# A transformer block on one core: the second MLP product with high and low weights side by side, and a batch's preparation spread over four chunk steps

## The chip, the cores and the metric

The kernel runs on one core of a Trainium2 chip. The metric is the device time of one execution in microseconds. Three executions of the kernel before gave 762.52 to 766.37 us, median 764.86.

The engines are called PE (TensorE; PEld is its loading of weights, the stationary operand), DVE (VectorE), ACT (ScalarE), POOL (GpSimd) and SP (SyncE, which here only issues DMAs). SBUF is the on-chip working memory, PSUM the memory in which matmuls accumulate; one PSUM bank holds 512 f32 columns per partition.

## What is computed

One block of a diffusion transformer for 16 batches of 256 tokens with 256 features: modulated self-attention, cross-attention to a context, and a modulated MLP with 1024 hidden features. The change touches only the MLP, which is the end of the reference:

```python
x = x + c_attn_out                                   # after cross-attention
x_norm2 = modulate(_ln(x), shift_m, scale_m)         # layernorm, times (1 + scale), plus shift
h = jax.nn.gelu(x_norm2 @ W_mlp1 + b_mlp1)           # 256 -> 1024, tanh form
h = h @ W_mlp2 + b_mlp2                              # 1024 -> 256
x = x + gate_m[:, None] * h
return x
```

All values are f32. The kernel multiplies in a reduced f32 format (fp32r) and gets the accuracy back by splitting: a value is a high part, rounded to the format, and a low part, the rest. A product a·b is then three matmuls: high·high, high·low and low·high.

## The kernel before

The attention of all batches comes first, as a pipeline of 32 units (16 self, 16 cross), written out by hand as steps (`beat`, L1037). Its results lie in DRAM as `x2d`. The last units run beside the start of the MLP; the order of that stretch is given by the lists in `E_` (L55), where `'M'` says at which half step the first three batches are loaded, biased, normalised and turned (L1003 to L1005).

After the attention, a loop over 64 chunks does the MLP (L1173 to L1193): 16 batches b of four chunks c, each chunk 256 hidden features. One round of that loop, the chunk step of (b, c), issues in this order, i being the chunk's number:

- `mlp_gelu` of chunk i + 1 (L837): ACT applies GELU twice to the first product in PSUM, into `hf` (f32, tag "pt", five buffers) and into `hh` (fp32r, the high part, three buffers); POOL subtracts into `hl`, the low part (three buffers)
- if c is 0, `mlp_T` of batch b + 1 (L800): PE turns the normalised tile `xn` by four transposes (`psT_m` in the trace), DVE scales into `xTf_m`, ACT writes the high part (into `wkch` or `wqch`, weights no longer needed), DVE subtracts into the low part (`wkcl`, `wqcl`)
- `mlp_first` of chunk i + 2 (L824): 12 matmuls of 256 columns into `ph`
- `mlp_second` of chunk i - 1 (L852): for each of two token tiles t, two 128-wide pieces of the hidden features and three matmuls, 12 in all, each with 128 x 128 stationary (a piece of `hh` or `hl`) and 256 columns of weights streaming. They accumulate over the batch's four chunks in `m.po`, the first 256 columns of a bank; batches alternate between the banks `sp` and `st`. In the trace these are `s<-big,hh`, `st<-big,hl` and so on. After a batch's last chunk, DVE multiplies the two tiles by the gate (`mt`), adds `xg` (`y`), and SP stores it
- at c = 1: `mlp_bias`, `mlp_stats` and `mlp_apply` of batch b + 2 (L1185 to L1188): POOL adds a bias to the loaded tile (`x<-x,cb`); DVE takes mean and variance (`st_m`, `mv_m`); POOL adds epsilon and takes the power -0.5 (`rs_m`, two small instructions, L289); DVE subtracts and multiplies (`xn_m`, two instructions of 256 columns, one per token tile)
- at c = 2: `mlp_residual` of b (L792): SP fetches the gate and gated bias (`gm`), DVE adds the latter to the tile (`xmg`)
- at c = 3: `mlp_load` of b + 3 (L775)

PE, DVE, POOL and SP issue in the order in which the program is written (L57, L58); ACT does so until chunk 23 and is ordered by the scheduler after that (L1174). So an instruction that waits holds up everything behind it on its engine.

The weights of the second product lie in `big[2]` (L871): eight pieces of 256 columns of high parts, then eight of low parts, so the high and low part of one piece lie 8 KB apart in each partition:

```python
W2 = [big[2][:, 0], big[2][:, 1]]
```

In the profile, nearly all instructions carry L51, the line of the helper that issues them, so they are told apart by their tiles.

Of the kernel before, what the change touches and what calls it, by code (L numbers as in the profile page):

```python
# [10 lines left out]
F32 = mybir.dt.float32  # L11
F32R = mybir.dt.float32r
AF = mybir.ActivationFunctionType
ALU = mybir.AluOpType
AX = mybir.AxisListType

P = 128
# [4 lines left out]
def pixart_block(  # L22
# [8 lines left out]
    B, N, H = x.shape  # L31
# [3 lines left out]
    NT = N // P  # L35
# [21 lines left out]
    PE = InOrder(nc.tensor, True)  # L57
    ACT, DVE, POOL, SP = (InOrder(e, True) for e in (nc.scalar, nc.vector, nc.gpsimd, nc.sync))  # L58

    const = ctx.enter_context(tc.tile_pool(name="const", bufs=1))  # L60
    work = ctx.enter_context(tc.tile_pool(name="work", bufs=2))
# [23 lines left out]
    big = [const.tile([P, 2, 8, N], F32R, name=f"big{i}") for i in range(3)]  # L85
# [15 lines left out]
    def tok(ap, b):  # L101
        return ap[b].rearrange("(t p) h -> p t h", p=P)
# [33 lines left out]
    st = psum.tile([P, 2, 512], F32, tag="st", name="st", bufs=1)  # L136
    sp = [psum.tile([P, 512], F32, tag=f"s{r}", name=f"s{r}", bufs=1) for r in range(2)]
# [134 lines left out]
    def layernorm(src, name):  # L272

        o = Box()

        def stats():
            o.st = work.tile([P, NT, 6], F32, tag="bnst", name=f"st_{name}")
            for t in range(NT):
                DVE.bn_stats(o.st[:, t], src()[:, t])

        def rstd(power=True):
            o.mv = work.tile([P, NT, 2], F32, tag="bnmv", name=f"mv_{name}")
            for t in range(NT):
                DVE.bn_aggr(o.mv[:, t], o.st[:, t])
            o.rs = work.tile([P, NT], F32, tag="rstd", name=f"rs_{name}")
            if power:
                o.pow()

        def pow():  # L289
            POOL.tensor_scalar(o.rs, o.mv[:, :, 1], EPS, None, ALU.add)  # L290
            POOL.tensor_tensor(o.rs, o.rs, mhalf, ALU.pow)

        def apply(eng=E_['LN'].get(name[0])):
            o.xn = work.tile([P, NT, H], F32, tag="xn", name=f"xn_{name}", bufs=3)
            if eng == "act":
                nb = work.tile([P, NT], F32, tag="nb", name=f"nb_{name}")
                DVE.scalar_tensor_tensor(nb, o.mv[:, :, 0], -1.0, o.rs, ALU.mult, ALU.mult)
            for t in range(NT):
                if eng == "act":
                    ACT.activation(o.xn[:, t], src()[:, t], AF.Identity, bias=nb[:, t:t + 1],  # L300
                                   scale=o.rs[:, t:t + 1])
                else:
                    (DVE if eng == "dve" else POOL).tensor_scalar(
                        o.xn[:, t], src()[:, t], o.mv[:, t, 0:1], o.rs[:, t:t + 1],
                        ALU.subtract, ALU.mult)

        o.steps, o.pow = [stats, rstd, apply], pow
        return o
# [103 lines left out]
    def mm3_tok(dst, xT, t, W, kn=KC, start=True, stop=True):  # L412
        n = 0
        for k in range(kn):
            for a, b in ((xT[0], W[0]), (xT[0], W[1]), (xT[1], W[0])):
                PE.matmul(dst, a[:, k, t * P:(t + 1) * P], b[:, k],
                          start=(start and n == 0), stop=(stop and n == 3 * kn - 1))
                n += 1
# [132 lines left out]
    def bc_t(ap):  # L551
        return ap.unsqueeze(1).to_broadcast([P, NT, H])
# [107 lines left out]
    def side(home, r):  # L660
        return home[r] if isinstance(home, (list, tuple)) else home[:, r]
# [111 lines left out]
    M = {}  # L773

    def mlp_load(b):  # L775
        m = M[b] = Box()
        m.h, m.hT = {}, {}
        m.xt = work.tile([P, NT, H], F32, tag="x", name=f"x2_{b}", bufs=5)
        SP.dma_start(m.xt, tok(X2d, b))
        m.ln = layernorm(lambda: m.xt, f"m{b}")  # L780

    def mlp_bias(b):
        POOL.tensor_tensor(M[b].xt, M[b].xt, bc_t(cb), ALU.add)

    def mlp_stats(b):
        M[b].ln.steps[0]()
        M[b].ln.steps[1]()

    def mlp_apply(b):
        M[b].ln.steps[2]("dve")  # L790

    def mlp_residual(b):  # L792
        m = M[b]
        m.g = work.tile([P, 2, H], F32, tag="g", name=f"gm_{b}", bufs=3)
        SP.dma_start(m.g.rearrange("p a h -> p (a h)"),
                     gd[b, 2:4].rearrange("a h -> (a h)").partition_broadcast(P))
        m.xg = work.tile([P, NT, H], F32, tag="xg", name=f"xmg_{b}")
        DVE.tensor_tensor(m.xg, m.xt, bc_t(m.g[:, 1]), ALU.add)

    def mlp_T(b):  # L800

        m = M[b]
        pst = ps_gen(f"psT_m{b}", SHORT)
        for f in range(KC):
            for t in range(NT):
                PE.transpose(pst[:, f * N + t * P:f * N + (t + 1) * P],
                             m.ln.xn[:, t, f * P:(f + 1) * P], ident)
        y = work.tile([P, KC, N], F32, tag="y", name=f"xTf_m{b}", bufs=2)
        hi, lo = (Wkc, Wqc)[b % 2]
        for f in range(KC):  # L810
            DVE.tensor_scalar(y[:, f], pst[:, f * N:(f + 1) * N], sc1[:, 1, f, b:b + 1],
                              cpT[:, 6 + f, b:b + 1], ALU.mult, ALU.add)
        if b in E_['DV']:
            DVE.tensor_copy(hi, y)
        else:
            for f in range(KC):
                ACT.activation(hi[:, f], pst[:, f * N:(f + 1) * N], AF.Identity,
                               bias=cpT[:, 6 + f, b:b + 1], scale=sc1[:, 1, f, b:b + 1])
        DVE.tensor_tensor(lo, y, hi, ALU.subtract)
        m.xT = (hi, lo)  # L820

    NCH = NF // 2
# [14 lines left out]
    def mlp_gelu(b, c):  # L837
        ph = M[b].h.pop(c)
        hf = work.tile([P, 2, N], F32, tag="pt", name=f"hf_{b}_{c}", bufs=5)
        hh = work.tile([P, 2, N], F32R, tag="qkh", name=f"hh_{b}_{c}", bufs=3)  # L840
        hl = work.tile([P, 2, N], F32R, tag="qkl", name=f"hl_{b}_{c}", bufs=3)
        for dst in (hf, hh):
            if b == 0:
                ACT.activation(dst, ph, AF.Gelu_apprx_tanh)
                continue
            for j in range(2):
                f = BM1 + 2 * c + j
                ACT.activation(dst[:, j], ph[:, j], AF.Gelu_apprx_tanh, bias=bT[:, f:f + 1])
        POOL.tensor_tensor(hl, hf, hh, ALU.subtract)
        M[b].hT[c] = (hh, hl)  # L850

    def mlp_second(b, c):  # L852
        m = M[b]
        hT = m.hT.pop(c)
        if c == 0:
            m.po = [side((sp, st)[b % 2], t)[:, :H] for t in range(NT)]
        for t in range(NT):
            mm3_tok(m.po[t], hT, t, [W2[0][:, 2 * c:2 * c + 2], W2[1][:, 2 * c:2 * c + 2]],
                    kn=2, start=(c == 0), stop=(c == NCH - 1))
        if c == NCH - 1:  # L860
            t1 = work.tile([P, NT, H], F32, tag="t1", name=f"mt_{b}")
            for t in range(NT):
                DVE.tensor_tensor(t1[:, t], m.po[t], m.g[:, 0], ALU.mult)
            y = work.tile([P, NT, H], F32, tag="x1", name=f"y_{b}", bufs=5)
            DVE.tensor_tensor(y, m.xg, t1, ALU.add)
            SP.dma_start(tok(out, b), y)


# [2 lines left out]
    W2 = [big[2][:, 0], big[2][:, 1]]  # L871
# [128 lines left out]
    def end(p, f, *a):  # L1000
        at_end[p // 16 - 1, p % 16].append(lambda: f(*a))

    for b, ps in enumerate(E_['M']):  # L1003
        for p, f in zip(ps, (mlp_load, mlp_bias, mlp_stats, mlp_apply, mlp_T)):
            end(p, f, b)  # L1005
    for c, p in enumerate(E_['H']):
        end(p, mlp_first, 0, c, (("c", 2), ("x1", 5))[c // 2])
# [165 lines left out]
    for i, (b, c) in enumerate(chunks):  # L1173
        ACT.on = i < E_['AP']  # L1174
        if i + 1 < len(chunks):
            mlp_gelu(*chunks[i + 1])
        if c == 0 and 0 < b < B - 1:
            mlp_T(b + 1)
        if i > 3 and i + 2 < len(chunks):
            mlp_first(*chunks[i + 2])  # L1180
        if i > 0:
            mlp_second(*chunks[i - 1])
        for _, f in zip(range(1), pst):
            f()
        if c == 1 and 2 < b + 2 < B:  # L1185
            mlp_bias(b + 2)
            mlp_stats(b + 2)
            mlp_apply(b + 2)  # L1188
        if c == 2:
            mlp_residual(b)  # L1190
        if c == 3 and b + 3 < B:
            mlp_load(b + 3)
    mlp_second(*chunks[-1])  # L1193


# [46 lines left out]
```

## Time and profile before

| what | value |
|---|---|
| median of three executions | 764.86 us (762.52 to 766.37) |
| the profiled execution | 765.13 us |
| its span, first to last instruction | 763.3 us |
| granted TensorE clock, mean | 0.999 |
| PE busy | 748.3 us, 10048 matmuls |
| DVE, ACT, POOL busy | 579.9, 563.3, 533.7 us |

The span is shorter than the execution's time by what lies around the first and last instruction. In rows of instructions stand: start and length in us (or a count and a mean), the engine, the operation, output<-inputs by name, the shape (for PE: contraction rows * output columns of the stationary operand, then partitions x columns), the count, and in brackets how long the engine was idle before and who released it. In rows of the chain of waits stand start, length and what ran.

### The profile page before, as it was taken

The page shows a single profiled execution, that of the slowest core. Times are in us where ns is not written, and L with a number is a line of the kernel's source. Part 1 is how long each engine was busy: PE and PEld are TensorE (multiplying, and loading weights), DVE is VectorE, ACT ScalarE, POOL GpSimd, SP SyncE. Part 2 cuts the span into 40 slices and gives each one's busy share as a digit, 9 for nine tenths or more (in the row PEclk, how much of TensorE's full clock was granted, in tenths as well). Part 3 has the DMA queues.
Part 4 walks back from the last instruction along what each step waited for, and adds up shares of the span by engine and source line. Part 5 has one row for each costly group of instructions (what it writes and reads, how often), then busy time and mean ns, then how long its engine had stood idle before and what let it go on. Part 6 is the DMA issues. An engine that isn't in the chain of part 4 may idle for free.

```text
span 763.3 us, 25123 instructions
## 1 busy us (share of the span) xinstructions
PE 748.3 (98%) x10048; PEld 653.4 (86%) x10048; DVE 579.9 (76%) x1214; ACT 563.3 (74%) x973; POOL 533.7 (70%) x553
## 2 busy tenths in 40 slices
PE   9999999999999999999999999999899999999997
PEld 8788878888888888888888888777689999999997
DVE  4888988888888888888888888887764565656652
ACT  4278888888888888888888888887657666666663
POOL 6767768696776968769687898854557666575653
PEclk9999999999999999999999999999999999999999
DMA  6554445436445354554545555445112222121211
GB/s 207 147 158 130 134 120 148 123 93 172 120 130 140 111 157 119 141 145 116 141 110 166 159 150 151 116 115 154 58 58 57 64 62 83 43 83 49 77 51 49
DMA packets 89049, 87.98 MB, mean 115 GB/s; under 512 B 8610, under 2 KB 84676, under 8 KB 88932
## 3 DMA queue, kind: packets, MB, share of 16 engines
q1 hardware_dynamic: 88468, 85.58, 40.0%
q8 instruction: 80, 1.31, 0.7%
q0 software_dynamic: 192, 0.52, 0.3%
q14 instruction: 37, 0.30, 0.1%
q10 hardware_dynamic: 272, 0.26, 0.1%
HBM read 26.97 MB, written 8.46 MB: 46 GB/s over the span
## 4 chain that ended last, share of the span: by engine, by line
PE 75%; DVE 9%; POOL 7%; ACT 6%; issue 1%; DMA 1%; POOLq 0%; ACTq 0%; DVEq 0%
PE o L51 15%; PE s L51 13%; PE st L51 11%; PE ps_qc L51 5%; DVE xn_m L51 5%; PE ps_q L51 4%; PE ps_kc L51 3%; PE ph L51 3%; PE ps_k L51 3%; PE ps_P_s L51 3%; POOL hl L51 3%; PE ps_v_c L51 2%; PE ps_v_s L51 2%; POOL x L51 2%; PE ps_P_c L51 2%; DVE xTf_m L51 2%
## 5 line engine op out<-in xcount | busy, mean ns | idle before, releaser
L51 DVE TENSOR_REDUCE mx<-s 128x2 f32<-128x512 f32 x504 | 325.0, 684 | 70.4 <-PE s L51 63.2
L51 ACT ACTIVATE pt<-st 128x1024 f32<-128x1024 f32 x252 | 258.9, 1027 | 23.9 <-PE st L51 15.8
L51 PE MATMUL s<-big 63*128 63x256 f32 (+1 forms) x1024 | 182.9, 298 | 0.6 <-issue 0.2
L51 PEld LDWEIGHTS s<-big 63*128 63x128 f32 (+1 forms) x1024 | 132.1, 186 | 19.8 <-DVE l_kc L51 6.6
L51 PE MATMUL st<-big 64*128 64x256 f32 (+1 forms) x1024 | 134.9, 300 | 3.7 <-ACT pt L51 3.7
L51 POOL TENSOR_TENSOR hl<-hf,hh 128x512 fp32r<-128x512 f32 x64 | 88.0, 1386 | 55.0 <-ACT hh L51 49.1
L51 PE MATMUL o<-pt,v 128*32 128x256 f32 x2048 | 123.8, 382 | 0.0
L51 PEld LDWEIGHTS st<-big 64*128 64x128 f32 (+1 forms) x1024 | 95.5, 186 | 21.4 <-issue 12.5
L51 PEld LDWEIGHTS o<-pt,v 128*32 128x32 f32 x2048 | 60.0, 109 | 41.5
L51 ACT ACTIVATE hf<-ph,bT 128x256 f32<-128x256 f32 x120 | 50.4, 474 | 27.0 <-PE ph L51 26.8
L51 ACT ACTIVATE hh<-ph,bT 128x256 fp32r<-128x256 f32 x120 | 50.5, 473 | 23.3 <-PE s L51 11.4
L51 ACT COPY oT<-o 128x512 f32<-128x512 f32 x63 | 37.0, 587 | 34.9 <-PE o L51 34.9
L51 PE MATMUL ph<-wqch,wself 128*128 128x256 f32 x256 | 51.5, 284 | 0.0
L51 PE MATMUL ph<-wkch,wself 128*128 128x256 f32 x256 | 51.3, 284 | 0.0
L51 DVE TENSOR_SCALAR xn_m<-x,mv_m,rs_m 128x256 f32<-128x256 f32 x32 | 37.2, 1202 | 15.3 <-POOL rs_m L51 15.3
L51 PE MATMUL s<-big,hh 128*128 128x256 f32 x256 | 46.7, 281 | 0.0
L51 PE MATMUL st<-big,hh 128*128 128x256 f32 x256 | 46.5, 281 | 0.0
L51 PE MATMUL ps_k<-xTh_s,wself 64*128 64x256 f32 (+1 forms) x232 | 43.9, 294 | 0.0
L51 PEld LDWEIGHTS ph<-wqch,wself 128*128 128x128 f32 x256 | 41.6, 189 | 0.4 <-issue 0.4
L51 PEld LDWEIGHTS ph<-wkch,wself 128*128 128x128 f32 x256 | 41.5, 189 | 0.2
L51 PE MATMUL ps_q<-xTh_s,wself 64*128 64x256 f32 (+1 forms) x240 | 40.1, 283 | 0.4 <-DVE l_q L51 0.4
L51 POOL TENSOR_SCALAR xn_c<-c,mv_c,rs_c 128x256 f32<-128x256 f32 x32 | 39.1, 1229 | 1.7
(228 smaller groups left out, 2464.7 us busy)
## 6 DMA issues: line engine op xcount, KB each, us to landing
big<-h_kc SPq DMA_DIRECT2D x64, 128.0 KB
big<-h_qc SPq DMA_DIRECT2D x64, 128.0 KB
big<-h_k SPq DMA_DIRECT2D x62, 128.0 KB
big<-h_q SPq DMA_DIRECT2D x62, 128.0 KB
big<-l_k SPq DMA_DIRECT2D x32, 128.0 KB
big<-l_q SPq DMA_DIRECT2D x32, 128.0 KB
c<-in_ctx_dram SPq DMA_DIRECT2D x16, 256.0 KB
g<-gd SPq DMA_DIRECT2D x16, 256.0 KB
```

The costliest lines, as they stand in the source:

```text
L51: i = f(*a, **k)
```

## The change

The second product streams a piece's high and low weights as one moving operand of 512 columns (two stretches of 256, 8 KB apart) past the high part of the activations, into a whole bank: high·high in the left half, high·low in the right half. The low part of the activations streams past the high weights, 256 columns, into the left half. The halves are added on DVE after the gate: one product of 512 columns per token tile, a sum that adds the right halves to `xg`, and the sum that made `y` before. The product's tile is now of tag "pt".

The preparation of batch b + 2 is spread: the bias at c = 0, the statistics and the fetch of the gate at c = 1, the power at c = 2, the normalisation and the residual at c = 3. The load of b + 3 goes to c = 1.

```diff
-    def mlp_stats(b):
+    def mlp_stats(b, power=False):
         M[b].ln.steps[0]()
-        M[b].ln.steps[1]()
+        M[b].ln.steps[1](power)
...
-    def mlp_residual(b):
+    def mlp_gates(b):
         m = M[b]
         m.g = work.tile([P, 2, H], F32, tag="g", name=f"gm_{b}", bufs=3)
         SP.dma_start(m.g.rearrange("p a h -> p (a h)"),
                      gd[b, 2:4].rearrange("a h -> (a h)").partition_broadcast(P))
+
+    def mlp_residual(b):
+        m = M[b]
         m.xg = work.tile([P, NT, H], F32, tag="xg", name=f"xmg_{b}")
         DVE.tensor_tensor(m.xg, m.xt, bc_t(m.g[:, 1]), ALU.add)
...
-            m.po = [side((sp, st)[b % 2], t)[:, :H] for t in range(NT)]
+            m.po = [side((sp, st)[b % 2], t) for t in range(NT)]
         for t in range(NT):
-            mm3_tok(m.po[t], hT, t, [W2[0][:, 2 * c:2 * c + 2], W2[1][:, 2 * c:2 * c + 2]],
-                    kn=2, start=(c == 0), stop=(c == NCH - 1))
+            for k in range(2):
+                for part in range(2):
+                    PE.matmul(m.po[t] if part == 0 else m.po[t][:, :H], hT[part][:, k, t * P:(t + 1) * P],
+                              big[2][:, :, 2 * c + k] if part == 0 else W2[0][:, 2 * c + k],
+                              start=(c == k == part == 0), stop=(c == NCH - 1 and k == part == 1),
+                              skip_group_check=True)
         if c == NCH - 1:
-            t1 = work.tile([P, NT, H], F32, tag="t1", name=f"mt_{b}")
+            t1 = work.tile([P, NT, 2, H], F32, tag="pt", name=f"mt_{b}", bufs=5)
             for t in range(NT):
-                DVE.tensor_tensor(t1[:, t], m.po[t], m.g[:, 0], ALU.mult)
+                DVE.tensor_tensor(t1[:, t], m.po[t].rearrange("p (a h) -> p a h", a=2), bc_t(m.g[:, 0]), ALU.mult)
+            DVE.tensor_tensor(m.xg, m.xg, t1[:, :, 1], ALU.add)
             y = work.tile([P, NT, H], F32, tag="x1", name=f"y_{b}", bufs=5)
-            DVE.tensor_tensor(y, m.xg, t1, ALU.add)
+            DVE.tensor_tensor(y, m.xg, t1[:, :, 0], ALU.add)
             SP.dma_start(tok(out, b), y)
...
-        if c == 1 and 2 < b + 2 < B:
-            mlp_bias(b + 2)
-            mlp_stats(b + 2)
-            mlp_apply(b + 2)
-        if c == 2:
+        ahead = b + 2 if 2 < b + 2 < B else None
+        if c == 0 and ahead:
+            mlp_bias(ahead)
+        if c == 1:
+            mlp_gates(b)
+            if ahead:
+                mlp_stats(ahead)
+            if b + 3 < B:
+                mlp_load(b + 3)
+        if c == 2 and ahead:
+            M[ahead].ln.pow()
+        if c == 3:
+            if ahead:
+                mlp_apply(ahead)
             mlp_residual(b)
-        if c == 3 and b + 3 < B:
-            mlp_load(b + 3)
```

The first three batches keep statistics and power together.

More of the change, by code (lines that the diff above doesn't have):

```diff
@@ L1003, in pixart_block @@
     for b, ps in enumerate(E_['M']):
-        for p, f in zip(ps, (mlp_load, mlp_bias, mlp_stats, mlp_apply, mlp_T)):
+        for p, f in zip(ps, (mlp_load, mlp_bias, lambda b: mlp_stats(b, True), mlp_apply, mlp_T)):
             end(p, f, b)
```

## The prediction

> **What bounds the kernel now.** I read the page first, then the stages, then the chain of waits inside the one stage that the diff touches.
>
> ```profile
> span 763.3 us, 25123 instructions
> ...
> PE 748.3 (98%) x10048; PEld 653.4 (86%) x10048; DVE 579.9 (76%) x1214; ACT 563.3 (74%) x973; POOL 533.7 (70%) x553
> ...
> PEclk9999999999999999999999999999999999999999
> ```
>
> The TensorE clock is granted in full throughout, and PE is never idle for long. A PE that is 98% busy isn't a PE that can't go faster, so the pace of its matmuls must be read. The stage table shows where the diff works; its columns are the stretch, its length, then the busy time and number of instructions of PE, PEld, DVE, ACT and POOL.
>
> ```profile
> 588.00:734.00 146.00, 144.03 (x1203) 141.27 (x1202) 88.08 (x157) 90.86 (x217) 92.58 (x85) 1.00 0.23 67
> ```
>
> DVE, ACT and POOL are some 60% busy here. The chain of waits (start, length, what) runs through all of them all the same:
>
> ```profile
> 588.00 2.68 DVE xn_m L51 x2
> ...
> 590.72 0.56 PE psT_m L51 x3
> 591.30 1.01 DVE xTf_m L51 x2
> ...
> 592.39 1.02 ACT wqch L51 x2
> ...
> 594.08 0.85 ACT hh L51 x2
> ...
> 595.05 1.72 POOL hl L51
> 596.77 1.26 POOL x L51
> 598.06 0.75 DVE st_m L51 x2
> ...
> 599.12 0.22 POOL rs_m L51
> ...
> 600.17 2.68 DVE xn_m L51 x2
> ...
> 733.89 2.68 DVE xn_m L51 x2
> ...
> 737.16 1.42 PE ph L51 x12
> ...
> 752.75 5.68 PE st L51 x48
> ```
>
> This is a ring, one turn per batch: normalise (xn), turn on PE, scale, high part, GELU, low part (hl), bias (x), statistics, rstd, normalise the batch after. From 588.00 to 733.89 it goes round twelve times: **12.16 us a batch**. PE itself needs less. A batch has 96 matmuls of 256 columns. The last 48 run without a gap in 5.68 us, 118.3 ns each, so 96 take 11.36 us. Then there are four turns:
>
> ```profile
> 650.87 0.28 PE L51 MATMUL s<-big,hl 128*128 128x256 f32 x1
> 650.99 0.27 PE L51 MATMUL psT_m<-ident,xn_m 128*128 128x128 f32 x1
> 651.44 0.55 PE L51 MATMUL psT_m<-ident,xn_m 128*128 128x128 f32 x3 [0.18 <-DVE xn_m L51]
> 651.74 0.36 PE L51 MATMUL ph<-wqch,wself 128*128 128x256 f32 x1
> 651.95 0.28 PE L51 MATMUL ph<-wqcl,wself 128*128 128x256 f32 x1
> ```
>
> The first turn starts at 650.99, the second not before 651.44, because the second half of xn isn't there. Three turns take 0.30 (651.44 to 651.74), the first would take 0.1, and the first matmul after them loses 0.1 (0.21 to the next start instead of 0.12). PE's need is 11.36 + 0.5 = 11.85 us, so it stands still 12.16 - 11.85 = **0.31 us a batch**. A second view of the same thing, who waited for xn over the whole run, and how long one xn takes:
>
> ```profile
> L51 DVE TENSOR_SCALAR xn_m<-x,mv_m,rs_m x32: 400/1374/1380, 546.7 to 735.2; 128x256 f32<-128x256 f32 x32
> ...
>   PEld psT_m L51: 5.3, 13
> ```
>
> 13 batches wait, 5.3 us in all by the weight loads, 13 x 0.31 = 4.0 by my account of PE. So the stage has two limits nearly level: PE's pace, and a ring 0.3 us longer.
>
> **Part 1, the wider matmuls.** Per chunk the second product has 12 matmuls of 256 columns; afterwards 4 of 512 and 4 of 256. The columns streamed stay the same (3072); four weight loads of 128 columns go. What a weight load costs shows where hardly anything is streamed:
>
> ```profile
> 9.95 0.97 PEld L51 LDWEIGHTS st<-sT,wf 128*128 128x128 f32 x8
> 10.06 0.96 PE L51 MATMUL st<-sT,wf 128*128 128x16 f32 x8
> ```
>
> Sixteen columns per matmul, yet the eight loads lie (0.97 - 0.19)/7 = 0.111 us apart (0.19 is one load's own length). A load-and-matmul pair therefore costs at least 0.11 us however little it streams. At 256 columns it costs 0.118. I read this as: 256 columns and a load are nearly level, and the load ends last. Then a 512-column matmul costs its columns only. No row shows what 256 columns take without a load beside them. It is no more than the 118 seen; since a bare load (111) and a full pair (118) lie so close, I put the columns level with the load's own time, 108, an estimate from the 111 less a handover. So **216 ns for the 512, 118 for the 256**: 334 instead of 3 x 118 = 354, so 20 ns a pair, 256 pairs (16 batches, 4 chunks, 4 pairs): **-5.1 us**. The bounds: columns alone set the pace (512 takes 236): 0. The 256 that follows also gets its load hidden behind the long stream and falls to 108: 354 - 324 = 30 ns, -7.7 us. The two halves of the moving operand lie 8 KB apart in one tile; no row shows such a stream, and I take it at nothing.
>
> [...]
>
> **Part 2, the ring.** Bias moves one chunk step ahead, statistics stay, the power goes behind the next hl, the normalisation two steps on. Bias and statistics thus leave the ring. What is late next? The power is now queued on POOL behind the fourth chunk's hl, and that waits for ACT's hh:
>
> ```profile
> 657.92 0.84 ACT L51 ACTIVATE hh<-ph,bT 128x256 fp32r<-128x256 f32 x2 [0.79 <-PE st L51]
> ...
> 660.48 0.84 ACT L51 ACTIVATE hh<-ph,bT 128x256 fp32r<-128x256 f32 x2 [0.52 <-PE st L51]
> ```
>
> Count from the first turn (650.99). This hh begins at +6.9 now; less 0.3 of standing and two second products shorter by 0.08 each, +6.45. It ends at +7.3, hl at +8.7 (1.3), rstd at +9.7 (0.22, 0.71 and two handovers). So the normalisation starts no earlier than today (660.81, +9.8): by its place alone the spreading brings nothing. What it changes is what runs beside it:
>
> ```profile
> 648.64 2.59 POOL L51 TENSOR_TENSOR hl<-hf,hh 128x512 fp32r<-128x512 f32 x2
> 648.71 2.67 DVE L51 TENSOR_SCALAR xn_m<-x,mv_m,rs_m 128x256 f32<-128x256 f32 x2 [1.14 <-POOL rs_m L51]
> 556.72 0.73 DVE L51 TENSOR_SCALAR xn_m<-x,mv_m,rs_m 128x256 f32<-128x256 f32 x2 [0.55 <-POOL rs_m L51]
> ```
>
> Today the POOL instruction before it waits for the statistics, two hl pile up, and both halves of xn run under them: 2.67 us, each half ending with an hl. In an earlier batch without that, the pair takes 0.73. Afterwards one of the two hl lies ahead of the power; the other's hh (660.48, +9.5) comes 0.3 and three shorter second products earlier and ends at about +9.8, hl can start at +9.9. The first half of xn runs free (+9.75 to +10.15); the second may be held by that hl to about +11.5. The turns come at +11.5 (11.85 less 16 x 0.02) and need the second half at +11.6. So no wait is left in the likely order: **-4.0 us** (between 0 and -5.3).
>
> [...]
>
> **Part 3, what is added.** On DVE a batch's two gate products grow to 512 columns and a 512-column sum comes in:
>
> ```profile
> 654.17 0.69 DVE L51 TENSOR_TENSOR wkcl<-xTf_m,wkch 128x512 fp32r<-128x512 f32 x1 [1.15 <-ACT wkch L51]
> 654.78 0.75 DVE L51 TENSOR_TENSOR mt<-s,gm 128x256 f32<-128x256 f32 x2
> 655.56 0.69 DVE L51 TENSOR_TENSOR y<-xmg,mt 128x512 f32<-128x512 f32 x1
> 658.70 0.75 DVE L51 BATCH_NORM_STATS2 st_m<-x 128x6 f32<-128x256 f32 x2 [2.44 <-POOL x L51]
> ```
>
> 0.75 becomes 1.35 (two of 0.69, overlapping a little), plus 0.69: +1.3 us of DVE per batch, hidden in the 2.44 us that DVE waits before the statistics. Those then end about 0.3 us ahead of the power; a cover that thin, if gone, delays rstd by as much. Bias on POOL now runs beside the low part (654.17), which is needed 2.3 us later. The gate's load and the next x load go out earlier on SP, one behind the other after the output store; both are used two steps later, so I put them at nothing. The new product tile takes every fifth buffer of "pt", with four hf between, so it comes back to its own slot.
>
> After the last batch nothing covers:
>
> ```profile
> 758.45 0.76 DVE L51 TENSOR_TENSOR mt<-st,gm 128x256 f32<-128x256 f32 x2 [1.04 <-PE st L51]
> 759.25 0.69 DVE L51 TENSOR_TENSOR y<-xmg,mt 128x512 f32<-128x512 f32 x1
> ```
>
> 1.48 us becomes 1.35 + 0.69 + 0.69 = 2.7: **+1.2 us**.
>
> **Sum**, against the profiled execution (765.13, that is the span and 1.8 around it): 765.13 - 5.1 - 4.0 + 1.2 = 757.2. The median is 0.27 lower, so **757.0 us**, 1.0% faster; new batch 11.5 us.
>
> **Rivals.**
> 1. Columns set PE's pace, 512 at twice 118: part 1 gives 0 to 11 ns a pair (11 if the handover is paid per matmul). For it: PE's rows show no pace at 512. Against: 0.111 us for 16 columns. Time 759.2 to 762.1.
> 2. The spreading doesn't do what it says: hl starts first, xn's first half is held to about +11.35 and its second ends at +11.7 or later, so PE still waits, 0.1 to 0.3 us a batch. For: xn starts only 0.15 us ahead of that hl by my count, and the power no earlier than today. Time 757.0 + 13 x 0.2 = 759.6, up to 761.
> 3. **Slower**: DVE becomes the bound, because its two-input sums are held by POOL. One was, elsewhere:
>
> ```profile
> 582.44 1.01 DVE L51 TENSOR_TENSOR y<-xmg,mt 128x512 f32<-128x512 f32 x1
> ...
> 581.57 1.34 POOL L51 TENSOR_TENSOR t_c<-t_c,x 128x512 f32<-128x512 f32 x1 [0.86 <-ACT t_c L51]
> ```
>
> DVE has 88.08/12 = 7.3 us a batch, less 1.9 of holding in xn, plus 1.3: 6.7. To exceed 12.16 its six exposed instructions (two xn, low part, two sums, residual) must be held 5.4 us, 0.9 each of a 1.3 us POOL instruction; at a full 1.3 each DVE needs 14.5 and the kernel 765 + 13 x 2.3 = 795. At 1.0 each, 12.7: 773. Against: only that one of sixteen y was held, for 0.3.
> 4. Both loads hide: 757.0 - 2.6 = 754.4.
>
> **How the numbers follow.** Forecast 0.48, rival 1 0.16, rival 2 0.18, rival 3 0.08, rival 4 0.10. A measurement here can tell 0.5%, 3.8 us, from no change; so faster means under 761.0. Forecast, rival 4, most of 2 and a quarter of 1 lie there: 0.77. Same 0.14, slower 0.09. The range, 753.5 to 762.2, takes in both bounds of part 1 and leaves out rival 3 and mixed mishaps.
>
> **What would show it.** Second-product pairs 334 ns apart (354 says rival 1, 324 rival 4). xn at 0.4 and 0.4 to 1.4 us, turns 0.11 apart, PEld's wait on xn near zero (rival 2 keeps it). A batch period of 11.5 us. DVE's two-input rows at 0.69; over 1 us in most batches says rival 3. The end from the last matmul to the output store 1.2 us longer. I am wrong if a 512-column stream split in two pieces costs more than two matmuls, or if the statistics, not hl, hold the power.

## The result and the profile after

The kernel after takes 765.81 us (median of 22 runs, 762.79 to 766.96), the kernel before 764.69 beside it (22 runs, 762.52 to 767.0). The ratio is **1.0007, 95% interval 0.9995 to 1.0018**: no change that can be measured, and 8.8 us above the forecast of 757.0. The profiled execution took 765.32 us. The page of the kernel after:

```profile
span 763.5 us, 24629 instructions
...
PE 747.0 (98%) x9792; PEld 642.7 (84%) x9792; DVE 602.6 (79%) x1230; ACT 563.0 (74%) x973; POOL 529.9 (69%) x553
```

The 256 matmuls fewer are there (9792 for 10048), and DVE has 22.7 us more to do (602.6 for 579.9), 1.4 a batch. PE is busy 1.3 us less. Nothing on this page tells where the gain went. The starts of xn do, in the rows of DVE of the kernel after (start, length):

```profile
564.79 1.04 DVE L51 TENSOR_SCALAR xn_m<-x,mv_m,rs_m 128x256 f32<-128x256 f32 x2
587.14 1.69 DVE L51 TENSOR_SCALAR xn_m<-x,mv_m,rs_m 128x256 f32<-128x256 f32 x2 [1.40 <-POOL rs_m L51]
614.49 1.82 DVE L51 TENSOR_SCALAR xn_m<-x,mv_m,rs_m 128x256 f32<-128x256 f32 x2 [2.17 <-POOL rs_m L51]
732.49 1.82 DVE L51 TENSOR_SCALAR xn_m<-x,mv_m,rs_m 128x256 f32<-128x256 f32 x2 [1.63 <-POOL rs_m L51]
```

These are batches 2, 3, 5 and 15, counted from 0. The same rows of the kernel before:

```profile
566.25 1.02 DVE L51 TENSOR_SCALAR xn_m<-x,mv_m,rs_m 128x256 f32<-128x256 f32 x2
...
612.26 2.67 DVE L51 TENSOR_SCALAR xn_m<-x,mv_m,rs_m 128x256 f32<-128x256 f32 x2 [1.14 <-POOL rs_m L51]
```

With 588.00 and 733.89 from the chain of before this gives the ledger. Last matmul means its end, 758.42 before and 756.52 after (start and length 758.14 + 0.28 and 756.24 + 0.28):

| stretch | before | after | difference |
|---|---|---|---|
| to xn of batch 2 | 566.25 | 564.79 | -1.46 |
| xn 2 to xn 3 | 21.75 | 22.35 | +0.60 |
| xn 3 to xn 5 | 24.26 | 27.35 | **+3.09** |
| xn 5 to xn 15, ten batches | 121.63 | 118.00 | **-3.63** |
| xn 15 to the last matmul | 24.53 | 24.03 | -0.50 |
| last matmul to the end of y | 1.52 | 3.61 | **+2.09** |

The first line is nearly all attention, which the change doesn't touch. The second and the fifth cancel: xn stands later in a batch's work. So there are three places to read: a gain in the steady batches, a loss in the first ones, a loss at the end.

**The steady batches.** 11.80 us instead of 12.16. Here PE never stands, which the rows of PE around a turn of the kernel after show:

```profile
639.88 0.40 PE L51 MATMUL st<-big,hh 128*128 128x512 f32 x1
640.12 0.28 PE L51 MATMUL st<-big,hl 128*128 128x256 f32 x1
640.24 0.60 PE L51 MATMUL psT_m<-ident,xn_m 128*128 128x128 f32 x4
```

The four turns come in one group, without the gap of before. But a pair takes 0.24 + 0.12 = 0.36 us, no less than three matmuls of 256 columns (3 x 118 = 354 ns). In the chain of waits whole second products stand side by side:

```profile
640.84 1.43 PE ph L51 x12
642.27 1.41 PE st L51 x8
```

Twelve matmuls of 256 columns take 1.43, the eight of the new form 1.41. The ring is gone, the wider matmul saves next to nothing.

The added sums cost little here either. The rows of the kernel after for the added sum and for `y`, all 16 batches (shortest/median/longest in ns):

```profile
L51 DVE TENSOR_TENSOR xmg<-xmg,mt x16: 691/808/1720, 581.4 to 758.7; 128x512 f32<-128x512 f32 x16
L51 DVE TENSOR_TENSOR y<-xmg,mt x16: 692/693/1669, 583.2 to 759.4; 128x512 f32<-128x512 f32 x16
```

`y` takes 1.67 us in batches 0, 1, 2 and 14, and 0.69 in the other twelve. In a steady batch it falls between two POOL instructions: one `y` runs from 634.66 to 635.35, an hl ends at 634.08 and the next begins at 635.67.

**The first batches.** The chain of the kernel after, where the loss of 3.09 lies:

```profile
582.60 1.18 POOL hl L51
...
586.36 4.27 DMA gm<-gd
...
590.66 0.97 DVE xmg L51
...
595.61 1.44 DVE xmg L51
...
597.07 1.67 DVE y L51
...
600.75 2.67 DVE xn_m L51 x2
...
603.47 0.90 PE psT_m L51 x3
```

Read it from the top. POOL's hl instructions hold `y` of batch 0, so its store goes late; on SP the gate of batch 1 (`gm`) is fetched behind that store and the store of the last attention result (`x2d`), and lands at 590.63. DVE, in order, stands at the residual (`xmg`) until then. What follows is late: the sums are held too (1.44 and 1.67 instead of 0.69), the statistics and xn come after them, and PE waits for xn. The turn that in the steady batches takes 0.1 us a piece is spread from 602.15 to 604.02. And the clock falls. The stage table of the kernel after (the last three columns are the granted clock, the DMA share and GB/s):

```profile
601.00:603.00 2.00, 0.43 (x2) 0.14 (x1) 2.00 (x2) 0.84 (x2) 1.95 (x2) 1.00 0.61 203
603.00:603.50 0.50, 0.04 (x1) 0.04 (x1) 0.50 (x2) 0.00 (x0) 0.26 (x1) 0.82 0.07 25
603.50:606.50 3.00, 3.00 (x14) 3.00 (x15) 1.51 (x3) 1.00 (x2) 1.41 (x1) 0.50 0.00 0
606.50:607.00 0.50, 0.50 (x4) 0.46 (x4) 0.45 (x1) 0.09 (x2) 0.00 (x0) 0.76 0.17 33
```

PE stands 1.57 + 0.46 = 2.03 us, and then runs at half its clock for some 3.4 us, which by the clock in the table costs an estimated 0.18 x 0.5 + 0.50 x 3 + 0.24 x 0.5 = 1.7. Two batches of 11.8 would be 23.6; 27.35 is 3.75 more, and that is 2.03 + 1.7. Of the changed kernel's 22 runs, six show a mean granted clock of 0.998 or more and take 762.8 to 764.1, the other sixteen 765.1 to 767.0; of 57 runs of the kernel before beside the experiments, 35 show 0.998 or more, median 764.1. With the clock granted the change is thus worth about 1.1 us (763.0, the median of the six, against 764.1). But the clock is lost in a second place too: in seven of the eleven traces of the experiments with the block (2, 3, 4, 7, 8, 11 and 12) the granted clock is 0.54 to 0.79 between 543.5 and 551 us, in the attention, which no edit touches; the traces of before and after show 1.00 there. Sorting the runs by their clock therefore takes out both losses. Where the clock was lost in the runs that have no trace is not shown.

**The end.** The chain of the kernel after:

```profile
750.93 1.67 DVE y L51
...
753.10 3.66 DMA gm<-gd
...
756.78 0.04 DVE xmg L51
...
757.39 1.29 DVE mt L51 x2
...
758.71 0.70 DVE xmg L51
...
759.44 0.69 DVE y L51
```

The same mechanism once more: `y` of batch 14 is held to 1.67, its store is late, the last gate fetch goes out at 753.10 behind it, and the last residual runs after PE has ended. PE ended at 756.52; the gate product begins at 757.39, some 0.8 us later than it could. The products of 512 columns and the added sum are the other 1.3.

### The profile page after: what moved, and what is told of

It reads as the page before. It is cut to its first block, busy times and chain, and to the rows that moved or that the text cites. A ratio compares the mean times of both kernels' runs of the same rounds, so it can differ in the third digit from the quotient of the medians.

```text
span 763.5 us, 24629 instructions
## 1 busy us (share of the span) xinstructions
PE 747.0 (98%) x9792; PEld 642.7 (84%) x9792; DVE 602.6 (79%) x1230; ACT 563.0 (74%) x973; POOL 529.9 (69%) x553
## 4 chain that ended last, share of the span: by engine, by line
PE 87%; DVE 5%; ACT 3%; POOL 2%; DMA 2%; issue 1%; SPq 0%; ACTq 0%; POOLq 0%; DVEq 0%
PE s L51 16%; PE o L51 14%; PE st L51 14%; PE ph L51 10%; PE ps_qc L51 4%; PE ps_q L51 4%; PE ps_kc L51 3%; PE ps_P_s L51 3%; PE ps_k L51 3%; PE ps_v_c L51 3%; PE ps_v_s L51 2%; PE ps_P_c L51 2%; DVE mx L51 1%; PE psA_c L51 1%; DMA gm<-gd 1%
## 5 line engine op out<-in xcount | busy, mean ns | idle before, releaser
L51 POOL TENSOR_TENSOR hl<-hf,hh 128x512 fp32r<-128x512 f32 x64 | 84.5, 1322 | 68.5 <-ACT hh L51 65.7
L51 PE MATMUL s<-big,hh 128*128 128x512 f32 x128 | 46.5, 397 | 0.0
L51 PE MATMUL st<-big,hh 128*128 128x512 f32 x128 | 46.3, 396 | 0.0
L51 DVE TENSOR_SCALAR xn_m<-x,mv_m,rs_m 128x256 f32<-128x256 f32 x32 | 27.0, 884 | 23.6 <-POOL rs_m L51 23.6
```

Of the source, the lines that this page charges most:

```text
L51: i = f(*a, **k)
```

## The experiments

After the traces the theory was: the spread opens the ring and is worth 4 to 5 us; the wide matmul saves nothing, because columns set PE's pace; its sums cost by POOL's holding and by the gate fetched behind a late store. The rivals: the spread does nothing by itself; the wide stream itself is slow (its two pieces 8 KB apart); the loss lies in the gate fetch alone.

**1. The wide product alone**, with the old preparation.

```diff
-            mm3_tok(m.po[t], hT, t, [W2[0][:, 2 * c:2 * c + 2], W2[1][:, 2 * c:2 * c + 2]],
...
+                    PE.matmul(m.po[t] if part == 0 else m.po[t][:, :H], hT[part][:, k, t * P:(t + 1) * P],
+                              big[2][:, :, 2 * c + k] if part == 0 else W2[0][:, 2 * c + k],
...
+            DVE.tensor_tensor(m.xg, m.xg, t1[:, :, 1], ALU.add)
+            DVE.tensor_tensor(y, m.xg, t1[:, :, 0], ALU.add)
```

> Only the 512-column matmuls and the sums that go with them; the preparation as before. Theory (PE's pace is set by columns, so the wide matmul saves next to nothing; the added DVE sums are held by POOL and cost in the first batches and at the end): batch period stays 12.1 to 12.3 us, pairs of 512 and 256 at 352 ns, end 1.2 us longer; 765.5 to 768 us. Rival (the wide matmul does save, and the spread preparation is what gives the time back): 760 to 762 us.

Measured: 779.17 us (775.47 to 783.25), ratio 1.0189 (1.0158 to 1.022), 14.5 us slower. I had not expected this. The groups of DVE from 588 to 734 in this kernel (count | busy us, mean ns | idle before):

```profile
L51 DVE TENSOR_TENSOR y<-xmg,mt 128x512 f32<-128x512 f32 x11 | 18.4, 1674 | 0.4
L51 DVE TENSOR_TENSOR xmg<-x,gm 128x512 f32<-128x512 f32 x11 | 18.3, 1660 | 1.0 <-DMA gm<-gd 0.9
L51 DVE TENSOR_TENSOR xmg<-xmg,mt 128x512 f32<-128x512 f32 x11 | 16.2, 1476 | 0.4
L51 DVE TENSOR_TENSOR mt<-st,gm 128x512 f32<-128x512 f32 x12 | 7.7, 683 | 0.0
```

These three instructions, which read two SBUF operands, are held for most of a POOL instruction; the gate product of the same size, which reads PSUM, is not (683). A fourth one with two SBUF operands, the low part (`wqcl`, `wkcl`), is not held either (0.69): POOL has nothing to do beside it. One turn of the ring that this makes, in the chain of the same kernel:

```profile
622.88 1.49 DVE xmg L51
...
624.39 1.68 DVE y L51
...
626.52 4.42 DMA gm<-gd
```

The held y sends the store late, the store the gate, the gate the residual, and DVE stands in between. The period of a batch is 13.5 us.

**2. The spread alone**, with the old second product.

```diff
-            m.po = [side((sp, st)[b % 2], t) for t in range(NT)]
+            m.po = [side((sp, st)[b % 2], t)[:, :H] for t in range(NT)]
...
+            mm3_tok(m.po[t], hT, t, [W2[0][:, 2 * c:2 * c + 2], W2[1][:, 2 * c:2 * c + 2]],
+                    kn=2, start=(c == 0), stop=(c == NCH - 1))
```

> Only the spread preparation; the second product as before, 256 columns and no added sums. Theory (the spreading opens the ring, and what was lost in the first batches and at the end comes from the added sums): batch period 11.85 us, no wait of 2.6 us for the fourth batch's turn, 760 to 761.5 us. Rival (the moved fetch of the gate and the moved residual cause the loss of the first batches by themselves): that wait stays, 763 to 764.5 us.

Measured: 759.82 us (759.1 to 761.64), ratio 0.9939 (0.9926 to 0.9953): 4.7 us faster. The stage table:

```profile
588.00:734.00 146.00, 146.00 (x1242) 146.00 (x1241) 94.98 (x162) 93.62 (x223) 90.79 (x86) 1.00 0.22 66
```

PE is busy for all of the 146 us. The rival that the spread does nothing falls. And since PE is also full in experiment 3 with the wide product, at the same pace, the wide product gives PE nothing.

**3. The change with the gate fetched a batch earlier.**

```diff
-        if c == 0 and ahead:
-            mlp_bias(ahead)
+        if c == 0:
+            if b == 0:
+                mlp_gates(0)
+            if ahead:
+                mlp_bias(ahead)
         if c == 1:
-            mlp_gates(b)
+            if b + 1 < B:
+                mlp_gates(b + 1)
```

> The changed kernel with each batch's gate fetched one batch earlier on SP. Theory (the residual waits for the gate's fetch, queued behind a late output store, and holds up DVE behind it): the 2.6 us wait at the fourth batch's turn shrinks below 1 us and the 0.9 us at the end goes; 761.5 to 763 us. Rival (the fetch only happened to come last; DVE is late from its held sums alone): as the changed kernel, 764.5 to 766 us.

Measured: 761.42 us (760.19 to 763.77), ratio 0.9954 (0.994 to 0.9969), 3.5 us faster than before and 4.4 faster than the kernel after (765.81), which is about what the first batches (3.75) and the late gate product at the end (0.8) cost together. The residual no longer waits for its gate, and the stand and the half clock at 601 to 607 are gone:

```profile
588.00:734.00 146.00, 145.95 (x1038) 136.44 (x1037) 103.80 (x176) 93.02 (x223) 92.29 (x88) 1.00 0.25 71
```

The loss in the first batches, then, is the gate behind the late store.

**4. The spread alone with the gate fetched earlier**, the edit of 3 on the kernel of 2.

```diff
+                mlp_gates(0)
...
-            mlp_gates(b)
+                mlp_gates(b + 1)
```

> The spread preparation alone, with each gate fetched one batch earlier. Theory: the ring is open and nothing waits for a gate: 760 to 761 us, at most 0.5 us under the spread preparation alone. Rival (the early fetch is what matters, with or without sums): 2 us or more under the spread preparation alone.

Measured: 760.44 us (759.01 to 761.76), ratio 0.9944 (0.993 to 0.9958), as 2. Without the added sums an early gate is worth nothing.

**5. The bias alone one chunk step earlier**, all else as before.

```diff
-        if c == 1 and 2 < b + 2 < B:
+        if c == 0 and 2 < b + 2 < B:
             mlp_bias(b + 2)
+        if c == 1 and 2 < b + 2 < B:
             mlp_stats(b + 2)
             mlp_apply(b + 2)
```

> The kernel before with one move alone: the bias one chunk step earlier; statistics, power and normalisation stay together at c = 1. Theory (the bias on POOL was the link that kept statistics late, and the ring is only 0.3 us longer than PE's need): taking it out opens the ring, batch period 11.8 us, 759.5 to 761 us, like the whole spreading. Rival (the later power and normalisation are what keeps xn clear of hl): no better than 763.5 us.

Measured: 759.35 us (759.27 to 761.31), ratio **0.9934** (0.9917 to 0.9951), 5.0 us faster: the lowest median of all kernels. Moving one POOL instruction gets all that the spread gets. Its chain in the steady part is PE's own work and nothing else:

```profile
648.02 0.44 PE psT_m L51 x4
648.46 1.43 PE ph L51 x12
649.89 1.42 PE s L51 x12
...
659.81 0.44 PE psT_m L51 x4
```

From turn to turn 11.79 us, with three matmuls of 256 where the kernel after has a pair and 11.80. That is the plainest measure of the wide product: nothing. DVE's y is held here too, and the residual waits for its gate:

```profile
L51 DVE TENSOR_TENSOR y<-xmg,mt 128x512 f32<-128x512 f32 x10 | 14.1, 1412 | 0.3
L51 DVE TENSOR_TENSOR xmg<-x,gm 128x512 f32<-128x512 f32 x11 | 11.4, 1040 | 10.1 <-DMA gm<-gd 10.1
```

1.0 us of waiting a batch (10.1 for about ten) that costs nothing, because DVE has room. The same holding is harmless or ruinous by what DVE has behind it. xn has room as well: it is done at 646.01 (644.32 + 1.69), 2.0 us before the turn at 648.02, where the kernel after has 0.3 us (638.09 + 1.82 = 639.91, turn at 640.24).

**6. The pace of PE by itself.** No block at all: series of 36 matmuls with a load each, while nothing is waited for.

```diff
+    series("same", alt(piece, 256))
+    series("line", alt(line, 512))
+    series("both", alt(both, 512))
+    series("pair", [m for i in range(18) for m in ((A[i % 4], both(i), 512), (A[(i + 1) % 4], piece(i), 256))])
+    series("short", alt(lambda i: piece(i)[:, :128], 128))
...
+    series("mid", alt(lambda i: flat[:, (i % 4) * 512:(i % 4) * 512 + 384], 384))
+    series("lean", [(A[i % 4][:, :32], piece(i), 256) for i in range(36)], 32)
+    series("leanline", [(A[i % 4][:, :32], line(i), 512) for i in range(36)], 32)
```

> No block at all: 11 series of 36 matmuls back to back after 60 to warm up, each with a load of its own and fp32r operands, nothing else busy; the output holds none of the block's values. Theory (columns set the pace): 256 columns 117 ns, 512 in one piece and in two pieces 234, 384 at 175, 256 with 32 stationary columns still 117; 128 and 64 columns are held up by the load, 107 to 112. Rival A (two pieces cost extra): 512 in one piece 216, in two pieces 234. Rival B (each load takes some of the stream's time): 256 with 32 stationary columns near 109, 512 in one piece near 225.

The program took 87.88 us. The chain gives each series as one row:

```profile
18.12 4.32 PE same L32 x36
22.44 8.19 PE line L32 x36
30.62 8.16 PE both L32 x36
38.78 6.35 PE pair L32 x36
45.13 3.97 PE short L32 x36
49.10 3.99 PE tiny L32 x36
53.09 7.90 PE mid L32 x36
61.00 4.24 PE lean L32 x36
65.24 8.33 PE leanline L32 x36
```

Divided by 36: 256 columns 120 ns, 512 columns in one piece 227.5, in two pieces 8 KB apart 226.7. So the split stream costs nothing. Eighteen pairs take 6.35, 353 ns each, against 3 x 120 = 360 in the same series and 354 in the kernel. 128 columns take 110 and 64 (`tiny`) 111, level with the 111 for 16 columns in the trace of before: there the load binds, and of these series only there. A stationary of 32 columns instead of 128 (in the kernel before, a load of 32 columns lasts 109 ns, one of 128 lasts 188) leaves 256 columns at 118 and 512 at 231. My reading that "the load ends last at 256 columns" is refuted. The series of 384 columns (`mid`) comes out at 219 ns each, not the 175 expected, because the granted clock was 0.50 for some 3.4 us of it; the last 18, at a clock of 1.00, take 3.12 us, 173 each. PE did not stand before that loss: two series of short matmuls (128 and 64 columns, 8 us in all) ran without a gap.

**7. The wide matmuls without the sums.** DVE evacuates the left half only, so high·low is left out.

```diff
-            t1 = work.tile([P, NT, 2, H], F32, tag="pt", name=f"mt_{b}", bufs=5)
+            t1 = work.tile([P, NT, H], F32, tag="t1", name=f"mt_{b}")
...
-            DVE.tensor_tensor(m.xg, m.xg, t1[:, :, 1], ALU.add)
...
-            DVE.tensor_tensor(y, m.xg, t1[:, :, 0], ALU.add)
+            DVE.tensor_tensor(y, m.xg, t1, ALU.add)
```

> The kernel before with the 512-column matmuls alone; DVE evacuates the left half as before and the right half (high activations times low weights) is left out of the result. Theory (the matmuls save next to nothing, the sums on DVE cost all of it): 764 to 766 us, batch period 12.1 to 12.2. Rival (the matmuls themselves cost, by weights read 8 KB apart or a longer wait for a batch's end): 768 us or more.

Measured: 764.52 us (763.48 to 766.48), ratio 1.0003 (0.9991 to 1.0014). The matmuls alone cost nothing. A gain on PE would hardly show here, since the ring still sets the pace (12.13 us a batch); that there is none is shown by 2 against 3 and by 5 against the kernel after.

**8. The sums without the wide matmuls**: 256 columns each, into two halves of the bank.

```diff
+                for n, (xp, wp) in enumerate(((0, 0), (0, 1), (1, 0))):
+                    PE.matmul(m.po[t][:, wp * H:(wp + 1) * H], hT[xp][:, k, t * P:(t + 1) * P],
+                              W2[wp][:, 2 * c + k],
```

> The kernel before with matmuls of 256 columns into two halves of the bank, and the changed kernel's gate products and sums. Theory (the sums on DVE cost all of it): like the wide matmul with its sums, batch period 13.4 to 13.6 us, 777 to 781 us. Rival (the matmuls cost): 766 to 768 us.

Measured: 780.36 us (772.76 to 783.13), ratio 1.0191 (1.0151 to 1.0232), y 1672 ns and the added sum 1477 as in 1. With 7, this puts the whole 14.5 us of experiment 1 on DVE's side of the change.

**9. The wide product with the bias one step earlier**, the edit of 5 on the kernel of 1.

```diff
-        if c == 1 and 2 < b + 2 < B:
+        if c == 0 and 2 < b + 2 < B:
             mlp_bias(b + 2)
```

> The wide matmuls and sums, with the bias alone one chunk step earlier. Theory (the early bias opens the ring; the sums then cost only where DVE is pressed, in the first batches and at the end): batch period near 11.8 us in most of the stage, 761 to 766 us, like the changed kernel. Rival (with the sums the whole spreading is needed, or DVE stays the bound): 770 us or more.

Measured: 765.61 us (763.28 to 768.4), ratio 1.0014 (0.9999 to 1.0029). That is the kernel after again: of the spread's moves the bias is the one that matters, with the sums as without them.

**10. Experiment 1 with POOL writing only**: `hl` is set to zero by two memsets.

```diff
-        POOL.tensor_tensor(hl, hf, hh, ALU.subtract)
+        for _ in range(2):
+            POOL.memset(hl.bitcast(F32), 0.0)
```

> The wide matmuls and sums with the old preparation, but POOL fills the low part of the activations with zeros, twice per chunk (two writes that read nothing, about as long together as the subtraction), so the low-by-high product is left out of the result. Theory (DVE's two-input instructions are held by POOL instructions that read SBUF): the sums, the residual and y at 0.69 us unless the bias runs, xn at 0.4, batch period 11.8 to 12.0, 760 to 763 us. Rival (DVE is late from its longer work, or held by whatever POOL does): rows of 1.4 to 1.7 us remain, 772 us or more.

Measured: 760.63 us (760.07 to 761.39), ratio 0.9952 (0.9934 to 0.997). y and the residual are back at 0.69, the added sum not (1.50, beside the bias, which reads). But these memsets don't wait for GELU, so the edit moves POOL's queue as well as its reads. Not clean.

**11. As 10, but POOL still waits for GELU**: it subtracts one column of each half first.

```diff
+        POOL.tensor_tensor(hl[:, :, :1], hf[:, :, :1], hh[:, :, :1], ALU.subtract)
         for _ in range(2):
-            POOL.memset(hl.bitcast(F32), 0.0)
+            POOL.memset(hl[:, :, 1:].bitcast(F32), 0.0)
```

> As the run with zeros, but POOL first subtracts one column of each half, so that it waits for GELU as it always does; then it fills the rest with zeros in two writes. The low-by-high product is left out but for two columns. This separates the reading of SBUF from the lost wait for GELU, which that run mixed up. Theory (DVE is held by POOL instructions that read SBUF, and the holding closes the ring): y and the residual at 0.69 us, batch period 11.8 to 12.4, 760 to 768 us. Rival (it was the lost wait that opened the ring): batch period 13 us or more, 772 us or more.

Measured: 762.42 us (760.15 to 762.81), ratio 0.9964 (0.9948 to 0.998). DVE's groups in this kernel, 600 to 720:

```profile
L51 DVE TENSOR_TENSOR xmg<-x,gm 128x512 f32<-128x512 f32 x11 | 7.5, 680 | 1.4 <-DMA gm<-gd 1.4
L51 DVE TENSOR_TENSOR xmg<-xmg,mt 128x512 f32<-128x512 f32 x10 | 6.9, 693 | 0.3
L51 DVE TENSOR_TENSOR y<-xmg,mt 128x512 f32<-128x512 f32 x10 | 6.9, 692 | 0.3
```

1660, 1476 and 1674 ns have become 680, 693 and 692, with POOL waiting for the same GELU and about as long at work for each hl (two memsets of 527 ns), only without reading. So it is not the time on POOL nor the wait that holds the sums, but POOL's subtraction, which reads SBUF. That the reading, and not something else in which a subtraction differs from a memset, is the reason, no run separates.

**12. Experiment 1 with the gate fetched earlier**, the edit of 3 in the old order.

```diff
+        if c == 0 and b == 0:
+            mlp_gates(0)
+        if c == 1 and b + 1 < B:
+            mlp_gates(b + 1)
         if c == 2:
             mlp_residual(b)
```

> The wide matmuls and sums with the old preparation, and each gate fetched one batch earlier. Theory (DVE itself, held, is the bound of this version; the gate's fetch only ends at the same time): 775 to 781 us, as without the early fetch. Rival (the ring runs through y, the output store, the fetch queued behind it and the residual): 770 us or less.

Measured: 772.36 us (771.81 to 772.52), ratio 1.0098 (1.0081 to 1.0116), between what the two theories gave. Of the 14.5 us the late gate is about 7 (779.17 - 772.36 = 6.8, with runs of experiment 1 up to 8 us apart); the 7.5 that are left (1.0098) are the held sums by themselves: the residual is back at 0.68, but

```profile
L51 DVE TENSOR_TENSOR y<-xmg,mt 128x512 f32<-128x512 f32 x9 | 15.0, 1670 | 0.3
```

and the statistics stand behind it in DVE's order. So the loss lies not in the gate fetch alone; both ways were real.

## Why the prediction was wrong

**Part 2, the ring: right.** Predicted -4.0, no wait left at the turns, xn's second half held by an hl. Measured: 0.36 us a batch, -3.6 in ten batches, and -4.7 and -5.0 for the spread and the bias alone. The period is 11.80, the 11.85 that was counted as PE's need. The count of the order comes out too, within 0.1 us, though the second products that it took to be shorter aren't: in the kernel after, xn starts 9.65 us after the first turn (649.89 - 640.24), where 9.75 was counted, and ends 1.82 later at +11.47, where +11.5 was. What I didn't see is that the bias alone does it; my count began with the power's place and not with what the bias had in front of it.

**Part 1, the step that failed first.** It said: "So 216 ns for the 512, 118 for the 256: 334 instead of 3 x 118 = 354", -5.1 us. Measured: 227 for the 512, 353 a pair alone, 352 in the kernel, at most 7 ns saved and nothing in the time. The reading of 111 for 16 columns and 118 for 256 as "nearly level, and the load ends last" was an inference from two limits that happen to lie close: by an estimate from experiment 6 loads set the pace up to some 230 columns (0.42 ns each and 12 on top reach the 110 of the short series there), columns beyond. The 108 for 256 columns without a load is close to what this slope gives (107.5); no run shows it, nor the handover that it took off the 111. What the prediction had wrong is the rest: the 12 ns on top are not the load ending last, for a matmul of 256 columns pays about as much with the load of 32 columns (118 against 120), and so does the one of 512 columns (227 for 215). Rival 1, at 0.16, was the case; it named the cause and the size (0 to 11 ns a pair). No row of the trace of before could tell the two apart, and the step deserved no more than even odds.

**Part 3, the step that failed second.** It said that the added 1.3 us of DVE work is "hidden in the 2.44 us that DVE waits before the statistics", and put the gate's fetch "at nothing". The work was sized right where it isn't held (at the end of experiment 3, two products of 1.30 together and two sums of 0.70 and 0.69: 2.7, as forecast). But the sums are not 0.69 when they stand next to POOL's hl: 1.4 to 1.7. Rival 3 named this holding and gave 773 to 795, and experiment 1 lies there (779). I gave it 0.08, since "only that one of sixteen y was held": a count that is true of the order of before alone: with the bias moved and nothing else (experiment 5) y is already held to 1.41, and in the kernel after four of sixteen are held to 1.67. By the sign set for it, rows over 1 us in most batches, rival 3 holds for experiment 1 and not for the kernel after. (Its lower end is 772 by its own numbers: 12.7 - 12.16, times 13, on 765.) What the rival had wrong is its condition: DVE doesn't need to be full (120.3 us of 146 in experiment 1). In-order waiting is enough: y late, store late, gate late, residual late, statistics late.

**The order saves it, mostly.** In the kernel after, the sums are hardly held from the fourth batch on (`y` 0.69 again, the added sum mostly 0.81), because `y` runs in the gap between two hl; the low part, which now runs beside the bias as the prediction said, takes about 1.3 instead of 0.69, and that costs nothing, for PE never stands there. So the change pays for its sums in the first batches (3.75 us) and at the end (2.1 where 1.2 was forecast, the difference being the gate), and not in between. Why the kernel leaves the bad regime after these batches isn't shown; that the late gate is what costs the time there is (experiment 3).

**The clock.** The prediction took it as granted in full. By the estimate above, 1.7 of the 3.75 us are a clock at half after PE stood for 2.0 us; a wait on PE was priced at its own length, and in this profile it cost nearly twice that.

Put together, against the sum of 757.2 for the profiled execution: part 1 saves nothing, +5.1; for the ring -4.0 was forecast, and -3.6 in ten batches with +3.1 in the first ones was found, +3.5; the end +0.9; the two stretches that cancel +0.1; the stretch up to xn of batch 2, nearly all of it attention, which ran ahead in this execution, -1.5 (four other traces at full clock there, those of 1, 5, 9 and 10, have that xn at 565.08 to 565.47). That is +8.1 and 765.3, as measured.

## What to carry over

Before adding an instruction to an engine that has idle time, look at where it reads from and what runs beside it on the other engine: a sum of two SBUF operands next to a GpSimd subtraction that reads SBUF is worth 1.7 us here, not 0.7 (next to memsets 0.69). Then follow what is queued behind it, through the DMA queue as well: the store that it feeds, and the load that is issued behind that store. And when two limits lie as close as 111 and 118 ns, measure each alone before building on which of them binds; the cheap part of a change (one moved POOL instruction, -5.0 us) may be all of it that pays.

## What the hardware showed that was not expected

- **The pace of a matmul in this format.** Between 256 and 512 columns it grows in experiment 6 by (227.5 - 120)/256 = 0.42 ns a column, with some 12 ns a matmul on top; 384 columns by that would take 173, and take 173 at full clock. The 12 ns aren't won back by merging two matmuls of a mix (353 ns a pair, where 227 + 120 would be 347). Why, no run here shows.
- **The clock fell after two short stands, and once after none.** In the kernel after, two stands of 1.1 and 1.0 us, with one matmul between them, were followed by about 3.4 us at a granted clock of 0.50. In experiment 6 it fell to 0.50 for as long with no stand at all; before that came 8 us of matmuls of 128 and 64 columns, one every 110 ns. What the clock goes by, no run here shows.
- **Holding goes by instruction, not by share.** Two-operand sums that begin while a POOL subtraction runs end some 0.55 us after it does (598.74 and 598.18 for `y` in the first batches of the kernel after; 0.69 becomes up to 1.77, in experiment 9); next to the POOL memsets of experiment 11 they take 0.69. It goes both ways: the bias takes 1.75 us in experiment 1, where it begins at 623.77 under a sum that began at 622.88 (1.78 on average in experiment 11), and 1.29 in experiment 10, where it begins first (652.70, the sum at 652.83). xn, which reads one SBUF operand, goes to 0.71 on average beside the memsets of experiment 11 and to 1.34 (2.67 for two) beside two subtractions.
